# Attention on one core: values made in four column tiles, key copies by halves, activations placed later, the last denominators in three parts

## The chip, the cores and the metric

The kernel runs on one core of one Trainium2 chip. The metric is device time in microseconds; a time below is the median of a kernel's runs, with the range beside it. TensorE multiplies matrices, ACT (ScalarE) and DVE (VectorE) do elementwise work, GpSimd (POOL in the profile) adds and issues some transfers, and the DMA engines move data. PSUM is the memory that TensorE's products go to; a bank is a piece of it. "Granted clock" is the share of full speed that TensorE was allowed. A "record" is one entry of TensorE in a trace; an fp32 matmul leaves two.

## The reference, cut to what matters

Sixteen images of 256 x 28 x 28 go through three layers of binary convolutions and then through attention over the 784 positions of each image. The change touches the attention only:

```python
xf = x.reshape(B, C, N)                          # B 16, C 256, N 784
q = jnp.einsum('rc,bcn->bnr', Wq, xf)            # r = 64
k = jnp.einsum('rc,bcn->brn', Wk, xf)
v = jnp.einsum('rc,bcn->bnr', Wv, xf)
attn = softmax(jnp.einsum('bnr,brm->bnm', q, k) / 8)
out = jnp.einsum('bnm,bmr->brn', attn, v)
return jnp.einsum('cr,brn->bcn', Wp, out) + x
```

The input x of the attention is itself unfinished when the attention begins: the last layer's scale, its residual ("p<-p,x" or a transfer "p<-x2d") and its prelu (a Relu of the negative part on ACT, then one fused DVE operation) are done image by image between the attention's own steps. The code calls these three `finish_a`, `finish_b` and `finish_c`.

## The kernel before

The attention works on keys in 7 chunks of 112. `x[b]` holds an image as two blocks of 128 channels. The pool "mi" has one pair of PSUM banks, so a query/key product and a projection that follow each other wait for each other's readers.

```python
def finish_a(b, n=slice(0, N)):
    for k in range(2):
        v = x[b][:, k, n]
        A.activation(v, v, AF.Identity, bias=bg3[:, k:k + 1], scale=sg3[:, k:k + 1])
        if b < 3:
            V.tensor_tensor(v, v, x2[b][:, k, n], ALU.add)
    if b >= 3:
        nc.gpsimd.dma_start(out=x[b], in_=x2d[b], accum_op=ALU.add)

def queries_keys(b):
    ps = two_banks(psmi, "mi")
    ...                                   # 4 matmuls into the two banks
    A.copy(k_[64:P], ps[64:P, :, :HN])
    for h in range(2):
        A.copy(q[64 * h:64 * h + 64], ps[0:64, h, :HN])
    V.tensor_copy(k_[0:64], ps[64:P, :, :HN])

def project_v(b):
    ps = one_bank(pssm, "sm")
    for c in range(NC_):                  # 7 chunks
        for k in range(2):
            T.matmul(ps[:MC, c * 64:(c + 1) * 64], lhsT=x[b][:, k, c * MC:(c + 1) * MC],
                     rhs=wv[:, k, :], start=(k == 0), stop=(k == 1))
    A.copy(va[b % 2][:, :, 0:64], ps[:MC, :NC_ * 64].rearrange("p (c r) -> p c r", r=64))
```

The loop over images runs in an order given by hand (cut; the branch for the last image is left out):

```python
for b in range(B):
    scores(b, 1); take_values(b - 1); project(b - 2, 0)
    sum_up(b, 1); scores(b, 2); sum_up(b - 1, 6); scores(b, 3); sum_up(b, 2, 3)
    watch(b - 2)                          # ACT: checks denominators
    finish_b(b + 2)                       # ACT: Relu of image b+2
    queries_keys(b + 1); project_v(b + 1); sum_all(b - 1)
    finish_c(b + 2)
    scores(b, 4); scores(b, 5)
    project(b - 2, 1); store(b - 2)
    sum_up(b, 5)
    finish_a(b + 3)
    ...                                   # values 0 to 3, denominators(b - 1), invert
    scores(b, 6); scores(b + 1, 0)
    ...                                   # values 4 to 6, normalize(b - 1)
```

`scores` are two matmuls and one exponential on ACT. `sum_up` adds exponentials, on GpSimd for chunks 0 to 3 and on DVE for 4 to 6. Ahead of the attention the kernel issues some idle matmuls, meant to keep TensorE's clock up; their start is where I begin to count the stages below.

## Time and profile before

| | before |
|---|---|
| time, median of 3 | 1140.85 us (1140.62 to 1141.15) |
| span of the profiled run | 1138.8 us |
| mean granted clock | 0.992 |
| first idle matmul to scores (1,1): "start" | 34.1 us |
| scores (1,1) to scores (15,1): "middle", 14 images | 245.7 us |
| scores (15,1) to the last addition: "tail" | 26.6 us |

Scores (b,c) are the score product of image b and chunk c, counted in order in the trace. The middle is where TensorE is never idle.

### The profile page before, as it was taken

Reading aid. Unit: us, or ns where it says so; the run is one execution under the profiler, and the core shown is the slowest. Engines: PE = TensorE matmul, PEld = TensorE weight load, DVE = VectorE, ACT = ScalarE, POOL = GpSimd, SP = SyncE. Lnnn points to the kernel's source line nnn. Section 1 sums busy time; section 2 is a strip of 40 time slices with the busy share of each in tenths; the row PEclk is TensorE's granted clock in tenths of the full one; section 3 lists DMA queues with packets and bytes.
Section 4 is the critical chain, followed back from the end, with each engine's and each line's share of the span. In section 5 each row is a group of like instructions: output and inputs, shape, how many; then the busy total and the mean of one; then the engine's idle time right before and its main releaser. Section 6 shows DMA issues by size and latency. Waiting matters only on the chain.

```text
span 1138.8 us, 15813 instructions
## 1 busy us (share of the span) xinstructions
PE 1109.4 (97%) x6067; PEld 944.5 (83%) x6067; DVE 802.2 (70%) x1431; ACT 711.5 (62%) x1054; POOL 136.2 (12%) x135
## 2 busy tenths in 40 slices
PE   7999999999999999998999999999999999999995
PEld 6999989999999999985999999999954554555542
DVE  4765378999999999956676564666664657667665
ACT  5655444777777777766555545555477776766742
POOL 2000000000000000000000000000023343443431
PEclk9999999999999999998999999999999999999998
DMA  8554331222222321014460000000014445354422
GB/s 329 199 174 155 129 127 43 80 77 100 100 85 74 125 86 57 30 56 157 178 271 1 1 1 1 1 1 1 1 57 114 132 123 164 104 158 144 112 85 87
DMA packets 26661, 111.63 MB, mean 98 GB/s; under 512 B 3458, under 2 KB 7236, under 8 KB 26580
## 3 DMA queue, kind: packets, MB, share of 16 engines
q1 hardware_dynamic: 21092, 80.82, 20.3%
q0 software_dynamic: 5488, 29.74, 8.8%
q8 instruction: 50, 0.82, 0.3%
q14 instruction: 31, 0.25, 0.1%
HBM read 65.59 MB, written 44.96 MB: 97 GB/s over the span
## 4 chain that ended last, share of the span: by engine, by line
PE 93%; DVE 4%; ACT 2%; issue 0%; DMA 0%; ACTq 0%; DVEq 0%; POOLq 0%
PE cv L254 33%; PE cv L598 25%; PE sc L1161 7%; PE av L1182 7%; PE mi L1146 4%; PE cv L704 4%; PE sm L1222 4%; PE cv L276 3%; PE unused L353 2%; PE mi L1232 2%; PE sm L1182 1%; PE sumabs L221 1%; PE hid L526 1%; PE gate L675 1%; DVE r L1207 0%
## 5 line engine op out<-in xcount | busy, mean ns | idle before, releaser
L598 PE MATMUL cv<-vs,w 128*128 128x392 f32 x1536 | 301.3, 354 | 0.0
L254 PE MATMUL cv<-fpads,wpk 128*128 128x392 f32 x1440 | 291.7, 355 | 8.0 <-DVE wpk L208 7.9
L598 PEld LDWEIGHTS cv<-vs,w 128*128 128x128 f32 x1536 | 287.0, 190 | 1.6 <-issue 0.3
L254 PEld LDWEIGHTS cv<-fpads,wpk 128*128 128x128 f32 x1440 | 270.7, 191 | 10.2 <-POOL worst L1043 7.9
L997 DVE SCALAR_TENSOR_TENSOR p<-r,r,cv 128x392 f32<-128x392 f32 x128 | 78.6, 614 | 78.4 <-ACT r L994 78.4
L1165 ACT ACTIVATE es<-sc 112x784 f32<-112x784 f32 x112 | 87.2, 822 | 73.9 <-PE sc L1161 73.7
L254 PE MATMUL cv<-fpads,wpl 128*128 128x392 f32 x576 | 124.9, 353 | 0.2 <-ACT t L268 0.2
L254 PEld LDWEIGHTS cv<-fpads,wpl 128*128 128x128 f32 x576 | 108.7, 190 | 1.1 <-ACT t L268 0.5
L268 ACT ACTIVATE t<-cv,rounding 128x392 f32<-128x392 f32 x96 | 56.1, 585 | 80.0 <-PE cv L254 77.6
L1161 PE MATMUL sc<-q,k 64*112 64x392 f32 x448 | 89.0, 510 | 2.6 <-DVE k L1153 1.6
L994 ACT ACTIVATE r<-cv 128x784 f32<-128x784 f32 (+1 forms) x66 | 52.9, 805 | 56.6 <-PE cv L276 55.2
L269 DVE TENSOR_SCALAR uv<-t 128x392 fp32r<-128x392 f32 x96 | 35.0, 364 | 71.4 <-ACT t L268 71.4
L1182 PE MATMUL av<-es,va 112*64 112x392 f32 x448 | 80.8, 499 | 0.0
L1161 PEld LDWEIGHTS sc<-q,k 64*112 64x112 f32 x448 | 35.8, 172 | 43.3 <-issue 18.3
L1182 PEld LDWEIGHTS av<-es,va 112*64 112x64 f32 x448 | 29.6, 136 | 47.4 <-issue 44.6
L1175 POOL TENSOR_TENSOR sum<-sum,es 112x784 f32<-112x784 f32 x32 | 68.4, 2138 | 2.6 <-POOL sum L1173 0.2
L103 DVE TENSOR_TENSOR vs<-pad 128x840 fp32r<-128x840 bf16 (+1 forms) x66 | 64.5, 1002 | 0.1
L1153 DVE COPY k<-mi 64x784 f32<-64x784 f32 x16 | 15.6, 976 | 64.2 <-ACT q L1152 64.2
L500 ACT CAST n<-cv 128x784 int16<-128x784 f32 x32 | 26.0, 812 | 54.4 <-issue 19.0
L1236 DVE TENSOR_TENSOR p<-mi,p 128x784 f32<-128x784 f32 x30 | 29.2, 975 | 31.5 <-PE mi L1232 31.1
L744 POOL DMA_DIRECT2D x2d<-x x16 | 8.5, 532 | 356.9 <-DVE x L738 294.1
L1222 PEld LDWEIGHTS sm<-wv,p 128*112 128x112 f32 x448 | 46.7, 178 | 4.9 <-issue 2.6
(254 smaller groups left out, 1714.4 us busy)
## 6 DMA issues: line engine op xcount, KB each, us to landing
xs<-in_x_dram SPq DMA_DIRECT2D x30, 784.0 KB, 4.4
x2d<-x POOLq DMA_DIRECT2D x16, 784.0 KB, 3.6
xd<-p SPq DMA_DIRECT2D x16, 784.0 KB, 3.3
out_dram<-p SPq DMA_DIRECT2D x15, 784.0 KB, 5.3
p<-x2d SPq DMA_DIRECT2D x13, 784.0 KB, 8.1
p<-x2d POOLq DMA_DIRECT2D x13, 784.0 KB, 9.1
n0d<-n POOLq DMA_DIRECT2D x16, 392.0 KB, 2.7
n<-n0d SPq DMA_DIRECT2D x16, 392.0 KB, 3.0
```

The source lines that it names most:

```text
L103: V.tensor_tensor(o, a, b, op)
L254: T.matmul(pss[j][:, mo, :HN].rearrange("p (a b) -> p a b", b=S), lhsT=lhsT, rhs=pads[:, j // 2 % 2, k, r:r + HR, c:c + S], start=start, s ...
L268: A.activation(r, pss[j][:, 0, :HN], AF.Identity, bias=rounding, scale=1.0 / PACK)
L598: T.matmul(ps.rearrange("p (a b) -> p a b", b=S), lhsT=w[:, k, c, u, mo * P:(mo + 1) * P], rhs=vs[:, b % 2, u, k, :, c:c + S], start=(n == 0),
L704: T.matmul(ps[:, h, :HN], lhsT=w[:, k, mo * P:(mo + 1) * P], rhs=z2[b][:, k, h * HN:(h + 1) * HN], start=(k + i == 0), stop=(k + i == 2),)
L994: A.activation(r[:, mo], ps[:, mo, :HN], AF.Relu, scale=-1.0)
L997: V.scalar_tensor_tensor(p, r[:, mo], beta[:, mo:mo + 1], ps[:, mo, :HN], ALU.mult, ALU.add)
L1161: T.matmul(ps[:MC, h, :HN], lhsT=k_[rows, c * MC:(c + 1) * MC], rhs=qs[b][rows], start=True, stop=True)
L1165: A.activation(e, ps[:MC, :, :HN], AF.Exp, scale=0.125)
L1175: (V if late else nc.gpsimd).tensor_tensor(sums[b, late], sums[b, late], e, ALU.add)
L1182: T.matmul(ps[64 * h:64 * h + 64, :HN], lhsT=w, rhs=e[:, h, :], start=start, stop=stop)
L1222: T.matmul(ps[:MC, c * 64:(c + 1) * 64], lhsT=x[b][:, k, c * MC:(c + 1) * MC], rhs=wv[:, k, :], start=(k == 0), stop=(k == 1),)
```

## The change

Four parts, as the diff has them.

1. v is made the other way round: the weights (32 of the 64 rows) stand still and quarter images of 196 positions stream, into four groups of 32 output partitions. A 32 x 32 transpose on DVE turns the result. For that, keys and values lie in blocks of 32 rows of which 28 are used; the rest is zero.
2. The key copies are taken by halves.
3. `finish_b` of image b+2 moves behind scores (b,5), the second projection of image b-2 and `watch` behind scores (b+1,0). On DVE the normalization of image b-1 moves forward, from behind the last values products to right behind its reciprocal. Image 2 gets its residual by an accumulating DMA as the later ones did. The start is ordered by hand too.
4. The last image has its own schedule; the denominators of the last two images are summed by TensorE in three parts, those of image 15 ahead of four of its values products (before, only image 15's were, behind all seven).

```diff
-            if b < 3:
+            if b < 2:
                 V.tensor_tensor(v, v, x2[b][:, k, n], ALU.add)
-        if b >= 3:
+        if b >= 2:
             nc.gpsimd.dma_start(out=x[b], in_=x2d[b], accum_op=ALU.add)
...
     def project_v(b):
         ps = one_bank(pssm, "sm")
-        for c in range(NC_):
+        for a in range(2):
             for k in range(2):
-                T.matmul(
-                    ps[:MC, c * 64:(c + 1) * 64], lhsT=x[b][:, k, c * MC:(c + 1) * MC], rhs=wv[:, k, :],
-                    start=(k == 0), stop=(k == 1),
-                )
-        A.copy(va[b % 2][:, :, 0:64], ...)
+                for g in range(4):
+                    T.matmul(
+                        ps[32 * g:32 * g + 32, a * GN:(a + 1) * GN], lhsT=wv[:, k, 32 * a:32 * a + 32],
+                        rhs=x[b][:, k, g * GN:(g + 1) * GN], start=(k == 0), stop=(k == 1),
+                    )
+        A.copy(vt[:, :, :, 0:GC]..., ps[:, 0:2 * GN]...)
+    def turn_v(b):
+        V.transpose(va[b % 2]..., vt...)
...
+        for b in range(B - 1):
             scores(b, 1)
+            if b == 0:
+                finish_b(1)
+                finish_c(1)
...
-            if b > 1:
-                watch(b - 2)
-            if b + 2 < B:
-                finish_b(b + 2)
...
+            if b == 0:
+                finish_a(2)
...
             scores(b, 5)
+            if b + 2 < B:
+                finish_b(b + 2)
+                finish_c(b + 2)
-            if b > 1:
-                project(b - 2, 1)
-                store(b - 2)
...
+                invert(b - 1)
+                normalize(b - 1)
+            scores(b, 6)
+            scores(b + 1, 0)
+            if b > 1:
+                project(b - 2, 1)
+                store(b - 2)
+            if b > 0:
+                watch(b - 1)
...
-                if b > 0:
-                    normalize(b - 1)
...
+        for c in range(3):
+            values(b, c)
         denominators(b)
+        for c in range(3, NC_):
+            values(b, c)
...
+        for mo, ps in enumerate((two_banks(psmi, "mi"), two_banks(pssc, "sc"))):
+            for n in parts:
+                project(b, mo, ps, n)
             store(b, slice(mo, mo + 1))
```

## The prediction

> **What bounds the kernel now.** I read the page first: busy shares, slices, chain, costliest groups. TensorE is busy 97% of the span, and the chain that ended last is TensorE for 93% of it.
>
> ```profile
> PE 1109.4 (97%) x6067; PEld 944.5 (83%) x6067; DVE 802.2 (70%) x1431; ACT 711.5 (62%) x1054; POOL 136.2 (12%) x135
> ...
> PE 93%; DVE 4%; ACT 2%; issue 0%; DMA 0%; ACTq 0%; DVEq 0%; POOLq 0%
> ```
>
> All edited code belongs to the attention stage, which starts at 836 us; the order listing moves nothing before the last normalization. So I then asked for busy time by stretch (columns: stretch, length, busy time of PE, weight loads, DVE, ACT, POOL, granted clock, DMA share, GB/s).
>
> ```profile
> 860.00:1106.00 246.00, 245.68 (x1452) 132.00 (x1450) 158.26 (x135) 169.86 (x270) 96.35 (x54) 1.00 0.46 127
> 1106.00:1139.00 33.00, 18.31 (x103) 8.18 (x102) 19.03 (x20) 9.50 (x25) 6.77 (x3) 0.83 0.19 76
> ```
>
> The middle 246 us (images 1 to 14) have no TensorE idle time worth naming, with DVE at 64% and ACT at 69%: there a microsecond off TensorE is a microsecond off the end, until another engine's loop takes over. The last 33 us are latency: TensorE works 18. One image takes 17.6 us. The timeline of TensorE for one (start, length, engine, line, tile):
>
> ```profile
> 967.87 2.90 PE L1146 MATMUL mi<-p,wqk 128*128 128x392 f32 x8
> 970.60 2.88 PE L1222 MATMUL sm<-wv,p 128*112 128x64 f32 x28
> 973.41 1.57 PE L1161 MATMUL sc<-q,k 64*112 64x392 f32 x8
> 974.82 0.93 PE L1232 MATMUL mi<-o,wp 64*128 64x392 f32 x4
> 975.68 2.85 PE L1182 MATMUL av<-es,va 112*64 112x392 f32 x16
> 978.36 0.83 PE L1182 MATMUL sm<-sum,ones 112*64 112x392 f32 x4
> ```
>
> To be read by differences of starts. An fp32 matmul is two records. The query/key product's 8 records take 970.60 - 967.87 = 2.73 us, so about 0.33 us per 392-column record with the whole array. The values product (av) has 16 records of the same width in 978.36 - 975.68 = 2.68 us, 0.17 each: its two halves write output partitions 0-63 and 64-127 and run side by side, two for the price of one. The projection of v (sm<-wv,p) takes 973.41 - 970.60 = 2.81 us for 28 records, 0.10 each, although each streams only 64 columns (0.33 x 64/392 = 0.054): it is held by its 112-column weight loads. Where the way of dividing the array changes, the gap to the next start grows by about 0.09 us.
>
> **What the Trainium skill says.** "TensorE: Matmul & The Clock Gate", Part 3, measured 2.38x for three 32-column tiles and says tiles in different column groups overlap. The trace agrees for two column groups (2x); four it doesn't show. "TensorEngine Tiling (Array Packing)", Key Properties: changing the tiling mode drains the engine; the 0.09 us above agree. "Vector Engine (DVE) Microarchitecture Reference", section 3.8, has the 32x32 transpose sustain one element per cycle per lane; no run here shows one yet. The TensorE page's Part 1 says an idle window of some 3.4 us halves the clock; the stretch 527 to 534 us, after two TensorE gaps of 1.25 and 0.61 us, agrees (granted clock 0.52).
>
> **Part 1, v in four column tiles.** Removed per image: 28 records, 2.81 us. Added: 16 matmuls = 32 records, 196 columns each, 32 output rows. A record alone: 0.33 x 196/392 = 0.165 us. If four column groups run together, 32 x 0.165 / 4 = 1.32 us; plus one more mode change (0.09) and its first load (about 0.1): 1.5 us. Saving 1.2 to 1.3 us per image.
> The copy out of PSUM stays (0.53 us before, 392 columns now). New: a DVE transpose of 448 columns, taken like a 392-column DVE operation (0.57), about 0.6 us.
>
> **Part 2, keys copied in halves.** ACT: two copies of 392 columns (0.48 each as the q copies) for one of 0.81, +0.15 us. DVE: two of about 0.57 for one of 0.98, +0.15. The score product now has 128 rows with zero padding; columns streamed and exp time (0.82) are unchanged. By the stretch above ACT comes to 169.86 / 14 + 0.15 = 12.3 us per image and DVE to 158.26 / 14 + 0.15 + 0.6 = 12.1: neither is full.
>
> But DVE's order matters. From the k copies, which follow ACT's last q copy, it now runs without a pause: copies 1.1, sum 1.0, transpose 0.6, sum 1.0, finishing 2.0, reciprocal 2.6, normalization 0.6, projection add 1.0 = 9.9 us, and that add frees the buffer for the next first projection. From that projection to ACT's last q copy: 0.66 + two scores 1.33 + 0.09 + q/k 2.8 + copies 1.45 = 6.3. A loop of 16.2 us beside TensorE's 17.6 - 1.25 = 16.35. Just hidden. Fourteen images at -1.2: **-17 us**.
>
> **Part 3, late activations, and image 2.** In the first image's loop the changed kernel scales image 2 on ACT, has the residual added by an accumulating DMA (it was a DVE add before), and then, still in the same iteration, puts that image's negative part (the Relu) on ACT ahead of the first image's last exp. The same pattern one image later in the kernel before:
>
> ```profile
> 854.66 1.97 ACT L1118 ACTIVATE p<-p,l2c_c,l2c_r 128x784 f32<-128x784 f32 x2
> ...
> 856.94 0.91 POOL L1122 DMA_DIRECT2D p<-x2d  x1 [5.28 <-ACT p L1118]
> ...
> 864.00 1.60 ACT L1128 ACTIVATE rl<-p 128x784 f32<-128x784 f32 x2
> ```
>
> There a whole image lies between issue and use, and the DMA landed 7 us after its issue (median 9.1 in the table of DMA issues). Now nothing does. Working forward from the first scaling at 832.3 with measured durations: first scores about 841.3 (843.2 before), q/k of image 1 end near 850, scaling of image 2 on ACT until about 854, exps 4 and 5 until 856, then ACT waits for the landing at about 861; Relu 1.7, scaling of image 3 2.05, exp 6 0.8 end at 865.5. TensorE runs out of work near 858.6 and takes the last values product at 865.6. Scores (1,1) start at about 866.2 instead of 860.2: **+6 us**. I add 0.45 because the transpose of the ones waits on DVE, inside the last normalization, for a longer row of memsets, and 2 us because 7 us of idle should cost some 4 us of half clock. Start in all: **+8.5**, less certain than the rest.
>
> **Part 4, the tail.** Timeline of TensorE at the end, with idle time ahead of each and what ended it:
>
> ```profile
> 1105.93 0.92 PE L1161 MATMUL sc<-q,k 64*112 64x392 f32 x4
> ...
> 1113.17 0.88 PE L1182 MATMUL sm<-sum,ones 112*64 112x392 f32 x4 [1.73 <-DVE sum L1178]
> ...
> 1118.83 0.93 PE L1232 MATMUL mi<-o,wp 64*128 64x392 f32 x4 [1.30 <-DVE o L1211]
> ...
> 1126.82 0.94 PE L1232 MATMUL sc<-o,wp 64*128 64x196 f32 x8 [1.95 <-DVE o L1211]
> 1130.25 1.68 PE L1232 MATMUL sc<-o,wp 64*128 64x196 f32 x8 [2.50 <-DVE o L1211]
> 1132.60 0.19 PE L1056 MATMUL count<-ones,ok 128*1 128x1 f32 x2 [0.67 <-DVE p L1236]
> ```
>
> From the last image's scores (15,1) at 1105.93 to the last add at 1132.55 are 26.6 us, 7.5 of them in these four gaps. New: image 14's denominators in three parts need no summing by DVE (the 1.73 gap goes; four pairs of records, 4 x 0.33 = 1.3 us of TensorE, come). Denominators of image 15 precede four of its values products, so the two half reciprocals (2.8) lie beside 2.6 us of TensorE. Counted from scores (15,1): ACT paces the scores until 7.3, projection 8.1, three values 10.2, denominators 12.2, four values 14.9, copy 15.6, normalization 16.3, two adds for image 14 18.2, four half adds of 0.56 20.5. So 20.5 for 26.6: **-6 us**. Stores and the final flag follow as before.
>
> **Sum.** -17 + 8.5 - 6 = -14.5: 1140.85 - 14.5 = about **1126 us**.
>
> **Rivals.**
> A: the four column groups don't overlap fourfold, because the two records of an fp32 matmul, or four streams from the same partitions, serialize them. For: only two groups have been seen. Against: the pairs start 7 ns apart at no cost. With two at a time the product takes 2.6 + 0.2 us, part 1 is worth nothing, and the time is about 1143.
> B: the wait for image 2's accumulation is hidden, or the scheduler's order hurts less than I think. Against: ACT's order has the Relu's wait ahead of exp 6, and no DMA of that kind in the trace landed in under 6.6 us. Time about 1117 to 1119.
> C: DVE becomes the bound. The loop above has 0.15 us to spare; a transpose of 1.2 us, or additions slowed by GpSimd at work (the 2.05 us sum against 0.97 for another in the same trace), would add 0.5 us per image: +7, about 1133.
>
> **Range and chances.** 2% faster is 1118. That needs B whole, or the clock to stay up and the tail and product both better than counted: 0.16. A and C together reach 1143 to 1150, not 1164: slower 0.03. Range 1116 to 1140: A's full failure (some 10%) lies above it, B's best below.
>
> **What would show it.** Per image, the v product at about 1.5 us and the spacing of query/key products at 16.3 to 16.5 instead of 17.6. Between 856 and 862 us, ACT idle with the accumulating DMA named as what ended it, and TensorE idle about 7 us before the first image's last values product, followed by a granted clock of 0.5. From scores (15,1) to the last add about 20.5 us. Waits of the projection for DVE's add in the middle stretch would mean C. A spacing near 17.6 with v at 2.8 us means A; no idle time near 858 us means B, and my start is wrong.

## The result, and the profile after

The changed kernel took 1133.64 us (1130.68 to 1135.18, four runs) against 1141.00 us (1140.62 to 1143.60) for the kernel before in the same rounds. The ratio is 0.9928, with a 95% interval of 0.9902 to 0.9953: a small gain, well clear of zero and inside 2%. Ratios here and below are the mean time of one kernel's runs over that of the other's of the same rounds, so not quite the ratio of the medians quoted.

The page of the changed kernel, its busy shares and its chain:

```profile
PE 1097.7 (97%) x6139; PEld 917.0 (81%) x6139; DVE 807.4 (71%) x1460; ACT 712.5 (63%) x1065; POOL 139.0 (12%) x140
...
PE 92%; DVE 3%; ACT 2%; issue 1%; DMA 1%; POOL 0%; SPq 0%; ACTq 0%; POOLq 0%; DVEq 0%
```

TensorE does 11.7 us less work than the 1109.4 of before. The span fell by 6.6. The chain now has 1% of DMA, where it had 0%, and GpSimd.

To see where the rest went I cut both traces at the same three instructions. Busy time by stretch, start, middle and tail, first of the kernel before (columns: stretch, length, then busy time of PE, weight loads, DVE, ACT, POOL, then granted clock, DMA share, GB/s):

```profile
826.11:860.19 34.08, 32.10 (x178) 17.30 (x177) 21.26 (x40) 25.97 (x39) 6.64 (x5) 1.00 0.23 79
860.19:1105.93 245.74, 245.41 (x1450) 131.94 (x1448) 158.26 (x135) 169.86 (x270) 96.35 (x54) 1.00 0.46 127
1105.93:1132.54 26.61, 18.19 (x102) 8.16 (x100) 18.88 (x19) 9.50 (x25) 6.77 (x3) 0.92 0.15 61
```

and of the changed kernel:

```profile
826.84:874.33 47.49, 35.59 (x186) 15.10 (x185) 24.20 (x43) 26.51 (x41) 8.94 (x8) 0.84 0.23 68
874.33:1103.98 229.65, 229.57 (x1507) 106.64 (x1505) 165.45 (x163) 172.00 (x288) 96.38 (x54) 1.00 0.48 134
1103.98:1125.99 22.01, 18.58 (x110) 8.26 (x108) 14.17 (x17) 7.80 (x16) 5.55 (x3) 0.99 0.30 122
```

| stage | before | after | change | predicted |
|---|---|---|---|---|
| up to the attention (same code) | 826.1 | 826.8 | +0.7 | 0 |
| start | 34.1 | 47.5 | +13.4 | +8.5 |
| middle | 245.7 | 229.65 | -16.1 | -17 |
| tail | 26.6 | 22.0 | -4.6 | -6 |
| last addition to the end | 6.2 | 6.2 | 0 | 0 |
| sum | | | -6.6 | -14.5 |

The middle gained what it should. The start gave most of it back: 13.4 us longer, with TensorE idle for 12 of its 47.5 us and a granted clock of 0.84.

**The middle.** TensorE's timeline for one image:

```profile
893.53 2.90 PE L1157 MATMUL mi<-p,wqk 128*128 128x392 f32 x8
896.36 1.53 PE L1243 MATMUL sm<-p,wv 128*32 128x196 f32 x32
897.82 1.59 PE L1180 MATMUL sc<-q,keyswa 64*128 64x392 f32 x8
...
909.93 2.24 PE L1157 MATMUL mi<-p,wqk 128*128 128x392 f32 x6
```

The v product takes 897.82 - 896.36 = 1.46 us where it took 2.81, and one image takes 909.93 - 893.53 = 16.40 us where it took 17.60. No idle time is shown on any of these lines.

**The start.** The timeline, TensorE, ACT, DVE and GpSimd mixed:

```profile
842.07 1.66 PE L1180 MATMUL sc<-q,keyswa 64*128 64x392 f32 x4 [2.37 <-issue]
843.65 2.44 PE L1243 MATMUL sm<-p,wv 128*32 128x196 f32 x32
...
848.60 4.55 DVE L1147 SCALAR_TENSOR_TENSOR p<-rl,na,p 128x784 f32<-128x784 f32 x2 [1.21 <-ACT rl L1142]
...
853.20 4.29 PE L1157 MATMUL mi<-p,wqk 128*128 128x392 f32 x6 [1.60 <-DVE p L1147]
...
861.68 0.91 POOL L1136 DMA_DIRECT2D p<-x2d  x1 [6.84 <-ACT p L1132]
...
868.61 1.60 ACT L1142 ACTIVATE rl<-p 128x784 f32<-128x784 f32 x2 [5.43 <-DMA p<-x2d]
...
872.83 1.57 PE L1201 MATMUL av<-es,v 128*64 128x392 f32 x4 [5.74 <-ACT es L1184]
```

Two things happen. The last three lines are the one foreseen: the accumulation into image 2 is issued at 861.68, ACT waits 5.43 us for it with its Relu, the exponential behind that Relu comes late, and TensorE is idle for 5.74 us. The lines above are the one not foreseen: DVE's two finishing operations of image 1 take 4.55 us together where such a pair takes 1.98 (869.49 in the same trace). The query/key product of image 1 waits for them twice (1.87 and 1.60 us) and then runs at half speed, 4.29 us for six records. The granted clock in stretches of the start:

```profile
842.00:845.60 3.60, 3.53 (x32) 1.71 (x36) 0.05 (x1) 1.75 (x2) 0.00 (x0) 0.53 0.00 0
...
852.70:859.30 6.60, 6.10 (x32) 3.04 (x35) 0.45 (x1) 1.75 (x4) 2.14 (x1) 0.51 0.30 122
```

After the gap of 2.37 us the first v product takes 2.37 us instead of 1.46 (not in every run: see "The last denominators behind all values"), and after the two waits for DVE the clock is halved for over 6 us of busy time. A third such stretch follows the wait for the DMA.

Why DVE was slow: the single operations in that timeline.

```profile
847.91 1.88 POOL L1192 TENSOR_TENSOR sum<-es 128x784 f32<-128x784 f32 x1 [16.79 <-ACT es L1184]
848.60 2.02 DVE L1147 SCALAR_TENSOR_TENSOR p<-rl,na,p 128x784 f32<-128x784 f32 x1 [1.21 <-ACT rl L1142]
850.17 2.15 POOL L1194 TENSOR_TENSOR sum<-sum,es 128x784 f32<-128x784 f32 x1 [0.38 <-ACT es L1184]
```

GpSimd's first sum ends at 849.79, DVE's first operation at 850.62, which is 0.83 us later. GpSimd's second sum ends at 852.32; DVE's second operation, which ends the pair at 853.15, is again 0.83 us behind. DVE began both while a sum ran and seems to have moved only once it ended. The Trainium skill says so in "SBUF — State Buffer", section "SBUF: two separate sides": a DVE operation with two SBUF inputs and a GpSimd operation that reads SBUF share a pair of ports, whichever starts first has it for its whole instruction, and the other blocks. The trace agrees with these two pairs. In the kernel before, this finishing took 1.03 us an operation, the last from 843.51 on, and GpSimd's first sum began only at 845.92.

**The tail.** TensorE at the end:

```profile
1119.92 0.82 PE L1259 MATMUL sc<-o,wp 64*128 64x392 f32 x4
1121.46 0.60 PE L1259 MATMUL mi<-o,wp 64*128 64x196 f32 x4 [0.71 <-DVE w__9465 L1054]
1123.03 0.60 PE L1259 MATMUL mi<-o,wp 64*128 64x196 f32 x4 [0.97 <-DVE p L1263]
...
1124.78 0.60 PE L1259 MATMUL sc<-o,wp 64*128 64x196 f32 x4 [0.81 <-DVE p L1263]
```

The second half of each projection of image 15 waits for DVE's addition of the first half (p, L1263), 0.97 and 0.81 us: the code projects one half, adds it, and projects the other into the same tile.

### The profile page after: what moved, and what is told of

It is laid out like the page before. It is cut to its first block, busy times and chain, and to the rows that moved or that the text cites. A ratio compares the mean times of both kernels' runs of the same rounds, so it can differ in the third digit from the quotient of the medians.

```text
span 1132.2 us, 16021 instructions
## 1 busy us (share of the span) xinstructions
PE 1097.7 (97%) x6139; PEld 917.0 (81%) x6139; DVE 807.4 (71%) x1460; ACT 712.5 (63%) x1065; POOL 139.0 (12%) x140
## 4 chain that ended last, share of the span: by engine, by line
PE 92%; DVE 3%; ACT 2%; issue 1%; DMA 1%; POOL 0%; SPq 0%; ACTq 0%; POOLq 0%; DVEq 0%
PE cv L255 33%; PE cv L599 25%; PE sc L1180 7%; PE av L1201 7%; PE cv L705 4%; PE mi L1157 4%; PE cv L277 3%; PE unused L354 2%; PE sm L1243 2%; PE mi L1259 2%; PE sm L1201 1%; PE sumabs L222 1%; DMA p<-x2d 1%; PE hid L527 1%; PE gate L676 1%
## 5 line engine op out<-in xcount | busy, mean ns | idle before, releaser
L1184 ACT ACTIVATE es<-sc 128x784 f32<-128x784 f32 x112 | 87.3, 822 | 23.9 <-PE sc L1180 23.0
L1180 PE MATMUL sc<-q,keyswa 64*128 64x392 f32 x448 | 91.6, 521 | 3.0 <-issue 2.4
L1201 PE MATMUL av<-es,v 128*64 128x392 f32 x448 | 81.6, 503 | 5.7 <-ACT es L1184 5.7
L1180 PEld LDWEIGHTS sc<-q,keyswa 64*128 64x128 f32 x448 | 39.5, 189 | 47.2 <-issue 27.8
L1201 PEld LDWEIGHTS av<-es,v 128*64 128x64 f32 x448 | 29.4, 137 | 53.4 <-issue 46.8
L1194 POOL TENSOR_TENSOR sum<-sum,es 128x784 f32<-128x784 f32 x32 | 68.0, 2126 | 3.4 <-ACT es L1184 1.0
L1168 DVE COPY keyswa<-mi 64x392 f32<-64x392 f32 x31 | 16.3, 564 | 56.0 <-ACT q L1164 56.0
L1157 PE MATMUL mi<-p,wqk 128*128 128x392 f32 x124 | 47.4, 525 | 3.5 <-DVE p L1147 3.5
L705 PE MATMUL cv<-z,fw 128*128 128x392 f32 x256 | 49.2, 343 | 0.8 <-ACT z L697 0.7
```

The costliest lines, as they stand in the source:

```text
L705: T.matmul(ps[:, h, :HN], lhsT=w[:, k, mo * P:(mo + 1) * P], rhs=z2[b][:, k, h * HN:(h + 1) * HN], start=(k + i == 0), stop=(k + i == 2),)
L1157: T.matmul(ps[:, h, :HN], lhsT=wqk[:, k, :], rhs=x[b][:, k, h * HN:(h + 1) * HN], start=(k == 0), stop=(k == 1))
L1180: T.matmul(ps[:, h, :HN], lhsT=chunk[rows], rhs=qs[b][rows], start=True, stop=True)
L1184: A.activation(e, ps[:, :, :HN], AF.Exp, scale=0.125)
L1194: (V if late else nc.gpsimd).tensor_tensor(sums[b, late], sums[b, late], e, ALU.add)
L1201: T.matmul(ps[64 * h:64 * h + 64, :HN], lhsT=w, rhs=e[:, h, :], start=start, stop=stop)
```

## The experiments

Eleven kernels were run, on three chips, each beside the kernel before (its median was 1140.7 to 1141.3 on all). All outputs are right. Stage times are of the one profiled run of each, cut as above. A difference between two starts is good to some 2 us: the start of the changed kernel took 47.5 us, and the same code 45.3 in the run "The last denominators behind all values". The times, of mostly four runs each, stand beside. My theory after the result: part 1 is worth its 16 us; the start loses 6 us to the transfer and some 5 to DVE behind GpSimd with the half clock that follows; the tail loses 1.6 to two waits. The rivals: that the gain of the middle came from the moved activations and not from the product; that the start lost its time to the hand-made order as a whole, or to the clock alone.

### The new product in the old order

The kernel before, with the changed layout, the key copies by halves, `project_v` and `turn_v`, and nothing moved:

```diff
+    keys = [wpool.tile([P, NC_, 4, 32], F32, ...) for t in ("wa", "wa2")]
...
+                for g in range(4):
+                    T.matmul(ps[32 * g:32 * g + 32, ...], lhsT=wv[:, k, 32 * a:32 * a + 32], ...)
...
                 project_v(b + 1)
                 if b > 0:
                     sum_all(b - 1)
+                turn_v(b + 1)
```

> The kernel before with the new layout alone (v in four column tiles and its transpose, key copies by halves into padded rows); order, start and tail as before. Theory: TensorE sets the middle, so the v product at 1.46 us for 2.81 takes 1.2 us per image off: query/key spacing 16.4, time about 1124 us. Rival (DVE's longer work or ACT become the bound in this order): spacing over 16.9 with waits on DVE in front of the projections, time over 1131.

Measured: 1141.14 us (1139.85 to 1144.65), ratio 1.0016 [0.9998, 1.0035]. The middle took 244.1 us, 17.55 per image. My expectation failed: the product took its 1.47 us (952.64 to 954.11), and 1.7 us of the middle was all that was gained. Where it went, by TensorE's waits over 205 us of the middle (engine, line, what it waited for: us in total, times, longest):

```profile
PE mi L1258 <- ACT es L1184: 11.4, 12, 1.6
```

Twelve images, 0.95 us each, ahead of the second projection; in the image shown next it is this line:

```profile
956.58 0.93 PE L1258 MATMUL mi<-o,wp 64*128 64x392 f32 x4 [0.89 <-ACT es L1184]
```

It is put down to an exponential, but the projection needs no exponential; by the code it needs the "mi" banks, whose last reader is DVE's copy of the keys. The same image on ACT and DVE:

```profile
951.90 1.59 ACT L1138 ACTIVATE rl<-p 128x784 f32<-128x784 f32 x2
953.51 0.86 ACT L1156 COPY keyswa<-mi 64x392 f32<-64x392 f32 x2
...
955.38 1.05 DVE L1156 COPY keyswa<-mi 64x392 f32<-64x392 f32 x2 [3.82 <-ACT q L1169]
```

DVE's copies end at 956.43, the projection starts at 956.58. They come that late because ACT has `watch` and the Relu of image b+2 ahead of the key and query copies; the query/key product had ended at about 952.6. The chain of waits from 949 to 983 us runs over those ACT operations in two images: scores, exponential, `watch`, Relu, copies, projection, and on to the next scores. In the image after, it reaches the Relu over GpSimd's sums and the accumulating transfer (10.72 us from issue to landing), for which ACT waited 0.6 us, once between 940 and 1010 us. In the kernel before the order on ACT was the same and its last query copy ended at 955.75; but there TensorE, with the longer v product, came to the projection only at 957.22 and did not wait.

### The new order with the old product

```diff
-    keys = [wpool.tile([P, NC_, 4, 32], F32, ...)]
+    keys = [wpool.tile([P, 2, HN], F32, ...)]
...
-        for a in range(2): ... 16 matmuls in four column groups
+        for c in range(NC_): ... 14 matmuls as before
     def turn_v(b):
-        V.transpose(...)
+        pass
```

> The changed kernel with the old layout of keys and v (v product in 28 records, no transpose), all order changes kept. Theory: the middle goes back to a spacing of 17.6, +17 us on the changed kernel: about 1150 us, so the order changes alone cost some 9 us against before (start +13, tail -4.6). Rival (the order changes themselves shorten the middle): spacing under 17.3, time under 1145.

Measured: 1151.74 us (1148.68 to 1151.91), ratio 1.0090 [1.0073, 1.0107]. Start 46.8, middle 246.3 (17.60 per image), tail 22.0. So the order alone is worth nothing in the middle, and costs the start and gains the tail what it does in the changed kernel. (The key copies by halves stay in this run too.) With the run before it, in the middle: the product alone -1.7 us, the order alone +0.6, both together -16.1. The middle's gain needs more than either.

### Image 2's residual by DVE again

```diff
-            if b < 2:
+            if b < 3:
...
-        if b >= 2:
+        if b >= 3:
...
-    for b in range(2):
+    for b in range(3):
         load_x2(b)
```

> The changed kernel, but image 2's residual added by DVE from a loaded copy, as before, not by an accumulating DMA. Theory: ACT's 5.4 us wait for the landing and TensorE's 5.7 us idle before the first image's last values product go, and with them the second stretch of half clock: 6 to 8 us faster, about 1126.5. Rival (that wait only covers lateness that the q/k product of image 1 causes anyway): under 3 us faster, over 1130.5.

Measured: 1125.15 us (1121.34 to 1128.41), ratio 0.9855 [0.9835, 0.9874]. The start fell from 47.5 to 41.0 us; ACT runs the Relu of image 2 without a wait:

```profile
864.34 1.60 ACT L1142 ACTIVATE rl<-p 128x784 f32<-128x784 f32 x2
```

The transfer's part is 6.5 us by this stage, within the 6 to 8 expected, and 8.5 by the median times.

### Image 1's finishing ahead of GpSimd's sums

```diff
         project_v(0)
+        finish_b(1)
+        finish_c(1)
         turn_v(0)
...
-            if b == 0:
-                finish_b(1)
-                finish_c(1)
```

> The changed kernel with image 1's negative part and its finishing on DVE placed ahead of scores (0,1), so before GpSimd's first sums; the accumulating DMA stays. Theory (GpSimd's sums slow DVE's finishing from 1.02 to 2.0 and 2.6 us, q/k of image 1 waits for that and then runs at half clock): finishing takes 1.0 each, the q/k product starts some 3.5 us earlier and at full clock, 4 to 6.5 us faster, 1127 to 1129.5. Rival (the slow finishing has another cause): durations stay at 2 us or more, time within 1.5 us of 1133.6.

Measured: 1129.31 us (1126.89 to 1132.52), ratio 0.9900 [0.9876, 0.9924]. The start took 42.7 us, 4.8 less, and the median time is 4.3 less. DVE in this run:

```profile
848.66 1.98 DVE L1147 SCALAR_TENSOR_TENSOR p<-rl,na,p 128x784 f32<-128x784 f32 x2 [0.98 <-ACT rl L1142]
```

1.98 us for the pair instead of 4.55, at nearly the same time, only that DVE comes first now: GpSimd's first sum starts at 850.17, inside the second operation, and it is the sum that takes longer, 2.21 us instead of 1.88. The query/key product of image 1 then ran its 8 records in one piece of 2.90 us, at full clock.

### Idle matmuls in the start's gaps

```diff
+    def keep_busy(n):
+        ps = one_bank(pssm, "sm")
+        for _ in range(n):
+            T.matmul(ps, lhsT=idle[:, 0:P], rhs=idle, start=True, stop=True)
...
+        keep_busy(10)
         scores(0, 0)
...
+            if b == 0:
+                keep_busy(14)          # ahead of image 1's query/key product
...
+                if b == 0 and c == NC_ - 1:
+                    keep_busy(22)      # ahead of the last values product
```

> The changed kernel with idle matmuls (10, 14 and 22 of 512 columns) put into TensorE's three idle stretches at the start: ahead of scores (0,0), of image 1's q/k product and of image 0's last values product. Nothing else moves. Theory: the half clock after those gaps costs real time (2.9 us at q/k and v of image 1, 1.5 at the end of image 0): no stretch of 0.5 clock at the start, 3 to 5 us faster, 1128.5 to 1130.5. Rival (the slow matmuls lie beside waits of other engines): within 1 us of 1133.6.

Measured: 1127.60 us (1125.16 to 1128.92), ratio 0.9865 [0.9844, 0.9886]. The start took 43.1 us, 4.4 less, though the waits for the DMA (5.33 us on ACT) and for DVE (4.56 us for the pair) were still there:

```profile
842.38 1.53 PE L1248 MATMUL sm<-p,wv 128*32 128x196 f32 x32
```

The first v product is at full clock, where it took 2.44 us in the changed kernel. By the median times the gain is 6.0 us, a little more than expected. So the clock by itself costs the start some 4 us, and it costs them because of the waits: the gain overlaps with that of the two runs above and is not to be added to theirs.

### The projection alone moved; the activations alone moved

Both start from the first experiment's kernel (new product, old order). One moves the second projection behind scores (b+1,0):

```diff
             scores(b, 5)
-            if b > 1:
+            if b > 1 and last:
                 project(b - 2, 1)
                 store(b - 2)
...
                 scores(b + 1, 0)
+                if b > 1:
+                    project(b - 2, 1)
+                    store(b - 2)
```

> The new layout in the old order, with the second projection of image b-2 and its store moved behind scores (b+1,0), as the change has it; ACT's order stays old. In the run without this move TensorE waited 0.9 us per image just ahead of that projection. Theory 1 (it waits there for the buffer that DVE's key copies free, and for nothing else): the wait goes, spacing 16.6, about 1128 us. Theory 2 (ACT's order closes a second loop: scaling, accumulating DMA of 9.9 us, Relu, copies, exps, next scaling; there the DMA landed only 0.6 us before its Relu): spacing can fall by 0.6 at most, 17.0, about 1133 us, with ACT waiting for the DMA.

Measured: 1133.73 us (1133.19 to 1137.14), ratio 0.9935 [0.9911, 0.9959]; the spacing of query/key products was 17.07 us and the middle took 237.4. That is the expected number of the second theory. Its mechanism, a loop through the accumulating transfer, I don't see: ACT waited for no transfer over 205 us of the middle. What TensorE waited for there:

```profile
PE mi L1258 <- DVE o L1230: 4.9, 12, 0.4
```

0.41 us per image for DVE's normalization, at the first projection. The chain of waits of this stretch goes from `watch` and the Relu on ACT to the key copies, then through DVE without a pause: key copies, sum, transpose, finishing, sum, reciprocal, addition, normalization. That is the DVE loop which the prediction had "just hidden", and it closes at 17.07 us here. That it does so because it begins behind two more ACT steps is argued, not shown: normalization also stands behind the addition of the late projection on DVE here, which takes 0.8 us (944.67 to 945.50), and the changed kernel puts it ahead.

The other moves `finish_b`, `finish_c` and `watch` only:

```diff
-            if b > 1:
-                watch(b - 2)
-            if b + 2 < B:
-                finish_b(b + 2)
...
             scores(b, 5)
+            if b + 2 < B:
+                finish_b(b + 2)
+                finish_c(b + 2)
...
                 scores(b + 1, 0)
+            if b > 0 and not last:
+                watch(b - 1)
```

> The new layout in the old order, projections left where they were, but ACT's Relu of image b+2 (with DVE's finishing) moved behind scores (b,5) and the watching copies behind scores (b+1,0). Theory: the late place of ACT's key and query copies is what kept the v saving from showing; with them 3 us earlier the buffer is free when the projection comes and the Relu has slack to the DMA: spacing 16.4 to 16.6, about 1125 us. Rival (the place of the projection matters): spacing over 17.2, over 1135.

Measured: 1132.52 us (1131.00 to 1134.58), ratio 0.9911 [0.9892, 0.9929]; spacing 16.94 us, middle 236.1. That lies between the two expected ranges. With the Relu gone from before them, DVE's key copies end at 955.50 and the projection starts at 955.65, 0.14 us behind its place, and then takes 0.27 longer: the bank is still freed a little late. So each move alone takes 6.7 and 8.0 us off the middle of the first experiment's kernel (244.1); added up they would give 229.4, and the changed kernel, with both, has 229.65. No run makes just these two moves, or moves the normalization alone: the changed kernel makes all three. Whether the late projection with the early normalization would do without the moves on ACT is untested.

### The start mended by two edits, and the tail's second halves issued early

The two edits of the start together, and in the tail:

```diff
             for n in parts:
-                project(b, mo, ps, n)
+                project(b, mo, ps, n, add=False)
+            for n in parts:
+                add_back(b, mo, ps, n)
             store(b, slice(mo, mo + 1))
```

> The changed kernel with both mends of the start (image 2's residual on DVE, image 1 finished before GpSimd's sums) and the last projections' half matmuls issued ahead of their half adds. Theory: the gains add, as they are two waits one after the other: 1125.15 - 4.3 - 1.4 = about 1119.5 us, scores (15,1) to last add 20.6 us instead of 22.0. Rival (both mends remove the same wait): about 1124.

Measured: 1119.53 us (1118.11 to 1121.79), ratio 0.9801 [0.9777, 0.9824]. Start 36.5, middle 229.0, tail 20.44. The projections of the tail are one piece each, with no wait of one for the other's addition:

```profile
1108.97 0.94 PE L1259 MATMUL mi<-o,wp 64*128 64x196 f32 x8 [0.72 <-DVE w__9468 L1054]
1109.71 0.86 PE L1259 MATMUL sc<-o,wp 64*128 64x196 f32 x8
```

The start is 11.0 us shorter than the changed kernel's, close to 6.5 and 4.8 added up, and the tail 1.6 shorter. The median time is 14.1 us less, where 8.5, 4.3 and 1.6 add up to 14.4. All as expected.

### The last denominators behind all values

```diff
-        for c in range(3):
+        for c in range(NC_):
             values(b, c)
         denominators(b)
-        for c in range(3, NC_):
-            values(b, c)
         take_values(b)
```

> The changed kernel with the last image's denominators put behind all seven of its values products instead of behind three; the same instructions. Theory (the tail gains because the two half reciprocals lie beside four values products): scores (15,1) to last add 24.4 us instead of 22.0, time about 1136. Rival (the tail's gain comes from the three parts alone and the place is indifferent): within 0.7 us of the changed kernel's tail.

Measured: 1134.51 us (1132.26 to 1136.70), ratio 0.9934 [0.9916, 0.9952]. The tail stage took 25.1 us instead of 22.0: the denominators began 13.1 us behind scores (15,1) instead of 10.5, and then came

```profile
1122.88 1.02 PE L1259 MATMUL mi<-o,wp 64*128 64x196 f32 x4 [2.66 <-DVE p L1263]
```

that is, an idle gap of 2.66 us where 0.71 stood, and half clock after it (four records in 1.02 us instead of 0.60). By the stage, the order of the last sums is worth some 3 us. By the times of the kernel it can't be said: it moved by 0.9 us, less than the spread of either kernel, and its profiled run had a start that happened to be 2.2 us shorter. That start is the same code as the changed kernel's, with the same gap ahead of scores (0,0), yet at full clock behind it:

```profile
843.35 0.93 PE L1180 MATMUL sc<-q,keyswa 64*128 64x392 f32 x4 [2.37 <-issue]
844.21 1.53 PE L1243 MATMUL sm<-p,wv 128*32 128x196 f32 x32
```

So the length of this gap alone does not decide whether the clock is halved.

### The v product, group by group

The same 16 matmuls, those of one column group together:

```diff
-        for a in range(2):
-            for k in range(2):
-                for g in range(4):
+        for g in range(4):
+            for a in range(2):
+                for k in range(2):
```

> The changed kernel with the loops of the v product turned round: all four matmuls of a column group one after the other, then the next group. Same instructions and data. Theory (TensorE starts matmuls in program order, so column tiles overlap only when neighbours use different groups): v takes about 4.8 us instead of 1.46, spacing 19.7, about 1183 us. Rival (it looks ahead past a busy column group): v stays near 1.5 us, 1133.6.

Measured: 1162.62 us (1161.92 and 1163.32, two runs), ratio 1.0187 [1.0168, 1.0206]. TensorE in the middle:

```profile
952.91 3.59 PE L1243 MATMUL sm<-p,wv 128*32 128x196 f32 x32
956.43 1.59 PE L1180 MATMUL sc<-q,keyswa 64*128 64x392 f32 x8
```

The product takes 956.43 - 952.91 = 3.52 us, the spacing is 18.45. Neither expectation hit it. Had it been served one by one, 32 records of 0.166 us would take 5.3 us; had TensorE reached past the records of a group to those of the next, 1.46. Within a group the records start 0.166 us apart. In the trace the second group's records begin after five of the first group's and then alternate with the rest of them. So matmuls of different groups do overlap, but only neighbours in the order of issue do; the four-fold overlap is owed to the inner loop over groups.

### The start mended further

Both edits of the start and the tail's, idle matmuls ahead of scores (0,0), and the scaling of image 3 moved behind scores (1,0):

```diff
+        keep_busy(10)
         scores(0, 0)
...
-            if b + 3 < B:
+            if 0 < b and b + 3 < B:
                 finish_a(b + 3)
...
             scores(b + 1, 0)
+            if b == 0:
+                finish_a(3)
```

> The kernel with both starts and the tail mended, plus ten idle matmuls ahead of scores (0,0) (keeps the clock over the first scores and v product) and the scaling of image 3 moved behind exps (0,6) and (1,0), which TensorE's last values product of image 0 waited 1.07 us for. Theory: 0.9 + 1.1 us less than 1119.5, about 1117.5, 2% below before. Rival: the waits move on, within 0.7 us of 1119.5.

Measured: 1119.77 us (1116.96 to 1120.46, five runs), ratio 0.9807 [0.9792, 0.9823]. In the profiled runs its start is 33.5 us, 3.0 shorter than with two edits, and shorter than before the change. The medians of the two kernels are the same within their spread all the same, so I don't claim a gain over the other. By the times the rival of this expectation holds, although the waits did go from the start. Both kernels are clearly faster than the kernel before, by 1.9 to 2.0%, and by their medians 1.2% faster than the changed one, which ran in other rounds.

## Why the prediction was right or wrong

The time (1126.0 predicted, 1133.64 measured) is inside its range, which was 24 us wide; the parts were not equally good. That the measured time is just the "about 1133" of rival C is luck: C did not come.

**Part 1, right in size, incomplete in cause.** v took 1.46 us (predicted 1.5), the spacing 16.40 (16.35), and the transpose 0.64 (0.6). Four groups ran four-fold, so rival A did not come, for the order of issue that the change chose: the group-by-group run shows what the other order costs. The middle's -16.1 instead of -17 is the half clock with which it began (granted 0.50 from 872.9 to 876.2 us); in the run with DVE's residual, where no wait precedes it, the middle is 228.9, 16.9 less than before. But the prediction credits the 17 us to the product alone, and part 3 nothing in the middle. The first two experiments refute that: there the product alone gave 1.7 us, and the order alone cost 0.6.

**Part 2, right.** DVE's key copies take 0.56 each and ACT's 0.48. ACT's busy time in the middle is 172.0 / 14 = 12.3 us per image (12.3 predicted), DVE's 165.45 / 14 = 11.8 (12.1). No run takes the halves away by themselves.

**Rival C did not come,** and the loop behind it is real: with `watch`, the Relu and the normalization at their old places, and the projection late, it closed at 17.07 us. In the changed kernel TensorE is busy for 229.57 of 229.65 us, so it is hidden.

**The step that failed: "Start in all: +8.5".** It was +13.4. Its wait for the transfer was right: ACT idle from 856 to 861 and TensorE for 7 us predicted, 5.43 and 5.74 us measured, with the landing 6.8 us after the issue; the run that takes the transfer away saves 6.5. (The +6 is not that wait but the whole shift of scores (1,1), from 860.2 to 866.2.) Rival B did not come. A term was missing: the finishing of image 1 was moved to run beside GpSimd's sums, took 4.55 us instead of 1.98, and halved the clock behind it, 4.8 us by the run that moves it ahead. I had the warning in hand, the DVE sum of 2.05 us against 0.97, and used it in rival C for the middle only. The clock term, 2 us and only after the long gap, was too small and in the wrong place: three stretches, the first after a gap of 2.37 us, and 4.4 us by the run with idle matmuls, much of it inside the 6.5 and 4.8. A warning stood in the trace before: at 527 to 534 us the granted clock was 0.52 after gaps of only 1.25 and 0.61 us. The prediction took this to agree with an idle window of some 3.4 us, which it does not. The whole sequence ran some 7 us later than I had reckoned, and nearly all of that was there before the transfer: the query/key product of image 1 was over at 857.4 instead of 850, and the landing came at 868.5 instead of 861. For the ones' transpose I had +0.45 us; no run singles it out.

**Part 4, the working short by one wait.** "Four half adds of 0.56" supposed the projections to be ready. They wait for the additions twice, 0.97 and 0.81 us; with them issued ahead the tail is 20.44 us for the 20.5 predicted. As it stands it is -4.6 for -6.

**Why a gain of 21 us became 7.** Middle and tail gave 20.7. The start took back 13.4, and 0.7 is the unchanged part before, which ended between 825 and 829 us in the profiled runs whatever the edit. Two small edits in the start and one in the tail take 12.6 us off these stages again (36.5 for 47.5 and 20.44 for 22.0).

The spread of a kernel's runs goes with the granted clock: the changed kernel's fastest run (1130.68 us) had 0.990 and the others (1133.16 to 1135.18) 0.985 to 0.986; with DVE's residual 1121.34 us had 0.995 and 1128.41 had 0.988. What stays open: what decides whether a gap is followed by half clock, how much each of the three half-clock stretches costs by itself, and which of the moves the middle needs.

## What to carry to other kernels

A product made cheaper on the bounding engine gives its time back only if the next thing that engine needs is free by then; look for the last reader of its buffer, and for what stands ahead of that reader on its own engine, because the wait is put down to whatever came last. In a steady loop an accumulating DMA or a GpSimd sum is hidden by distance; at the loop's first round the distance is missing, so walk through that round alone. And matmuls that are to run side by side in column groups must alternate in the order of issue.

## What the Trainium skill lacked or had wrong

- "TensorE: Matmul & The Clock Gate", Part 3, gives 2.38x for three column tiles, and no measurement for four. Here four column groups of fp32 matmuls ran four-fold: 32 records of 0.166 us (an estimated 5.3 us one after another) in 1.46 us with the change of tiling included, which is 3.6x.
- No page says what the order of issue does to that overlap. With the groups' matmuls adjacent the same 32 records took 3.52 us; only neighbouring groups overlapped.
- "TensorE: Matmul & The Clock Gate", Part 1, has the clock halved after an idle window of some 3.4 us. Here it was halved after a gap of 2.37 us (granted 0.53 in the 3.6 us behind it), while the same gap in another run of the same code left it at 1.00, and so did a gap of 1.55 us at nearly the same place in the kernel before. What decides it no run shows.
- "SBUF — State Buffer" has the port shared by DVE and GpSimd right, but no figure for elementwise DVE work: here a finishing operation of 1.03 us took 2.02 and 2.60 us.
- No page has the time from issue to landing of an accumulating DMA of 784 KB: 6.8 us after its issue in the start, a median of 8.3 in the changed kernel.
